# A shorter scan warm-up, A u as its own product, and zero products between scan steps

## The chip, the cores and the metric

The kernel runs on one core of one Trainium2 chip. The metric is the device time of one execution in microseconds (us), lower is better. The core has the engines PE (matrix products, with its weight loads listed as PEld), DVE (VectorE), ACT (ScalarE), POOL (GpSimd) and SP (which issues DMAs). PE's granted clock is given as a share of full speed; it is either 1.0 or 0.5 in a given window of 3.41 us.

## The reference

One block: layer norm, cross attention with 8 heads, a second layer norm, and a small state-space recurrence over 4096 positions, whose output is added to the residual. Cut to what matters here (T = 4096 positions, 3202 keys, H = 512, state S = 64):

```python
x  = residual + _mha(layernorm(x), layernorm(ctx), W_qkv, b_qkv, W_o, b_o)
xn = layernorm(x)
U  = (xn @ W_in.T + b_in) @ Bmat              # 4096 x 64

def step(s, u_t):
    s = silu(s @ A.T) + u_t
    return (s, s)
_, states = scan(step, zeros, U)              # one after the other, 4096 steps

x  = x + states @ Cmat
return x + (program_probs.mean(axis=1) @ W_prog.T + b_prog)
```

silu(z) is z times the logistic function of z; with z = 2 z', it is z' (tanh(z') + 1), which is what the kernel computes.

## The kernel before

**Attention.** The queries are 8 blocks of 512; a unit is one block, one pair of heads and one half (256 queries), 64 units in all. Each unit takes 13 chunks of 2 x 124 keys. For a chunk PE makes scores (L464), ACT copies them (L474), DVE keeps a running maximum (L485), later DVE subtracts the maximum (L519), ACT takes the exponent (L529), POOL accumulates the sums (L538) and PE multiplies by V (L547). The 832 steps (unit, chunk) are written out in one loop over g (L945), in which the later stages run some 16 steps behind the scores. For the last unit the sums of even chunks are made on PE instead (L563), those of odd chunks on POOL.

**The drain.** After the last scores (k = g - 832 counts from 0) only the subtract, exponent and V products of the last unit are left, with the scan's first steps put in at the values k of SCAN_AT (L940). fetch (L740) brings in, for k = 1 to 16, the rows of the residual that the output will be added to; last_fetch (L747) the constants.

**The projection.** finish, project (L623) and its copy for the last 256 rows, last_rows (L850), form x1 = residual + attention output (L859, L867), its layer norm, the transposes (L140) and u = 2 (W x + b) (L884, L891). For all rows but the last 256, u is ready before the drain.

**The scan.** It isn't run over 4096 steps. The positions are cut into 256 chunks of L = 16, 128 of them on the lower 64 partitions and 128 on the upper, so one step of all chunks is one product of 128 x 128 with a block-diagonal A. What a chunk starts from is found by running ahead: main_scan (L829) runs

- WARM = the last 8 steps of each chunk from the u before them (sweep at L837),
- a full sweep of 16 steps from the ends of the chunks to the left (L839),
- a second full sweep (L841), which also makes the output: products (L800, s @ Cmat, two products of 64 x 128 x 512) and outputs (ACT L805, DVE L806 and POOL L810 add them to the row, SP sends it out).

At the end, differ compares the two sweeps' ends; where they differ by more than 2^-21 of the maximum, a repair loop runs (under the condition at L1028). A step (L776) is the product z = A s (L778), tanh (L780), h = (tanh + 1) z (L781) and s = h + u (L782), each waiting for the one before.

**The last rows.** The last 256 positions have their u late, so they are a scan of their own (last_rows from L898): chunks of LT = 8 with PRE = 24 steps run ahead. Here z = A u is one product for all steps at first (zl, L900) and A h is added to it (L910), so a step needs no addition of u. Its 32 steps run beside the main scan's sweeps. last_outputs (L921) multiplies them by Cmat and adds.

**What sets the order.** Everything from L942 is a manual schedule: an engine executes its instructions in the order in which the program records them. Generators (`yield`) interleave last_rows with the scan, one scan step for each piece. When last_rows is exhausted, the rest of the scan runs alone (L1014), then last_outputs, the comparison and the end.

PSUM: z has two halves of 4 steps; py has two pairs of banks.

Of the kernel before, what the change touches and what calls it, by code (L numbers as in the profile page):

```python
# [8 lines left out]
F32 = mybir.dt.float32  # L9
BF16 = mybir.dt.bfloat16  # L10
I32 = mybir.dt.int32
AF = mybir.ActivationFunctionType
ALU = mybir.AluOpType
# [15 lines left out]
LAG = 3  # L29
EPS = 1e-5  # L30
L = 16
WARM = 8
LT = 8
PRE = 3 * LT
NCK = T // L // 2
TOL = 2.0**-21

# [10 lines left out]
def xattn_ssm_kernel(  # L48
# [34 lines left out]

    ident = const.tile([P, P], F32, name="ident")
    make_identity(nc, ident)
    ones = const.tile([P, HD], F32, name="ones")
    nc.vector.memset(ones, 1.0)
    neg_half = const.tile([P, 1], F32, name="neg_half")
# [482 lines left out]
    def finish_last(w):  # L571
        Q, hp, half = w["at"]
        o = op.tile([P, QU], F32, tag="o", name=f"o_{Q}_{hp}_{half}", bufs=12)
        o_t[Q, hp, half] = o
        nc.scalar.copy(o, w["po"][:, 0, :])
        sums(w["pd"], w["acc"], CK, False, True)
        yield
        rd = op.tile([P, QU], F32, tag="rd", name="rd_last", bufs=1)
        for t in range(2):
            nc.vector.reciprocal(  # L580
                rd[:, t * P : (t + 1) * P], w["pd"][:, t * P : (t + 1) * P]
            )
        nc.vector.tensor_tensor(o, o, rd, ALU.mult)
        yield

    def finish(w):

# [143 lines left out]

    x1r = x1d.rearrange("(v c j) o -> v j c o", v=2, j=L)
    outr = out.rearrange("(v c j) o -> v j c o", v=2, j=L)
    counts = (NCK, END)
# [10 lines left out]
    def last_fetch():  # L747

        for g in range(2):
            r = LAST + g * P  # L750
            t = xp_.tile([P, H], F32, tag="x", name=f"xr_{r}", bufs=3)
            nc.sync.dma_start(t, x[r : r + P, :])
            xl.append(t)
        t = qp.tile([P, QB], F32, tag="q", name="c2")
        for k in (0, NS):
            nc.sync.dma_start(t[k : k + NS], cmat)
        sv["c2"] = t
        one = sp_.tile([P, 8, NCK], F32, tag="s", name="scan_1")
        sv["th"] = [one[:, i, :] for i in range(2)]
        sv["h"] = [one[:, 2 + i, :] for i in range(2)]  # L760
        sv["s"] = [one[:, 4 + i, :] for i in range(3)]
        sv["ok"] = one[:, 7, :]
        two = sp_.tile([P, 1024], F32, tag="s", name="scan_2")
        at_ = 0
        for name, n in (
            ("end0", NCK + 1), ("end1", NCK + 1), ("ul", PRE + 1 + P), ("hw", P), ("hl", P),
            ("sl", P + 1), ("df", NCK), ("thl", P // LT), ("st", P // LT),
            ("top", 1), ("bad", 1), ("badl", 1),
        ):
            sv[name] = two[:, at_ : at_ + n]  # L770
            at_ += n
        assert at_ <= 1024
        for g in range(2):
            nc.gpsimd.tensor_tensor(xl[g], xl[g], rowb, ALU.add)

    def step(j, before, s, z):  # L776

        nc.tensor.matmul(z, a_t, before, start=True, stop=True)  # L778
        th, h = sv["th"][j % 2], sv["h"][j % 2]
        nc.scalar.activation(th, z, AF.Tanh, scale=0.5)  # L780
        nc.vector.scalar_tensor_tensor(h, th, 1.0, z, ALU.add, ALU.mult)  # L781
        nc.vector.tensor_tensor(s, h, u[:, j, :], ALU.add)  # L782

    def zs(j):
        return sv["z"][:, j // 4 % 2, j % 4, :]

    def sweep(first, start, end):

        before = start
        for j in range(first, L):  # L790
            s = end[:, 1:] if j == L - 1 else sv["s"][j % 3]
            step(j, before, s, zs(j))
            before = s
            yield j, s
        nc.vector.tensor_copy(end[NS:, 0:1], end[:NS, NCK : NCK + 1])

    def products(j, s):
        for v, n in enumerate(counts):
# [30 lines left out]
    def main_scan():  # L829
        ends = sv["end0"], sv["end1"]  # L830
        sv["z"] = ps_s.tile([P, 2, 4, NCK], F32, tag="s", name="z")
        for end in ends:
            nc.vector.memset(end[:NS, 0:1], 0.0)

        n = PRE + 1 - L
        nc.vector.tensor_copy(sv["ul"][:NS, :n], u[NS:, L - n :, END - 2])
        nc.vector.tensor_copy(sv["ul"][:NS, n : PRE + 1], u[NS:, :, END - 1])  # L837
        for _ in sweep(L - WARM, u[:, L - WARM - 1, :], ends[0]):
            yield  # L839
        for _ in sweep(0, ends[0][:, :NCK], ends[1]):  # L840
            yield  # L841
        for j, s in sweep(0, ends[1][:, :NCK], ends[0]):
            yield
            products(j, s)
            outputs(j)
            yield
        differ(ends[0][:, 1:], ends[1][:, 1:], NCK, sv["bad"])
        yield

    def last_rows(w):  # L850

        yield from finish_last(w)
        Q, tiles = NQB - 1, range(2)
        pas, x1s, scaled, xns = [], [], [], []
        for g in tiles:
            pa = ps_m.tile([P, H], F32, tag="m", name=f"pa_l{g}")
            pas.append(pa)
            for c in range(NC):
                nc.tensor.matmul(  # L859
                    pa, o_t[Q, c, 1][:, g * P : (g + 1) * P], wo[:, c, :],  # L860
                    start=(c == 0), stop=(c == NC - 1),
                )
            yield
        for g in tiles:
            x1 = xp_.tile([P, H], F32, tag="x1", name=f"x1_l{g}")
            x1s.append(x1)
            nc.vector.tensor_tensor(x1, pas[g], xl[g], ALU.add)  # L867
            scaled.append(normalize(x1, P, f"yl{g}", later=True))
            yield
        tps = []  # L870
        for g in tiles:
            xh = scaled[g]()
            tps.append(transposes(ps_m, "m", xh, P, f"yl{g}"))
            nc.gpsimd.tensor_tensor(xl[g], x1s[g], modb, ALU.add)
            yield
        pus = []
        for g in tiles:
            xn = sv["xn"][:, g, :].rearrange("p (c k) -> p c k", c=NC)
            nc.scalar.copy(xn, tps[g])
            hs = slice(g * NS, (g + 1) * NS)  # L880
            pu = ps_m.tile([P, P], F32, tag="m", name=f"pu_l{g}")
            pus.append(pu)
            for c in range(NC):
                nc.tensor.matmul(  # L884
                    pu[hs], wc[:, c, :], xn[:, c, :], start=(c == 0), stop=(c == NC - 1)
                )
            yield
        ul, hw, hl, sl, th = (sv[k] for k in ("ul", "hw", "hl", "sl", "thl"))
        for g in tiles:
            hs = slice(g * NS, (g + 1) * NS)  # L890
            nc.vector.tensor_scalar(  # L891
                ul[hs, PRE + 1 :], pus[g][hs], bu[hs], 2.0, ALU.add, ALU.mult
            )
            if g == 0:
                nc.vector.tensor_copy(ul[NS:, : PRE + 1], ul[:NS, P:])
            nc.sync.dma_start(x1d[LAST + g * P : LAST + (g + 1) * P, :], xl[g])

        zl = ps_m.tile([P, PRE // LT + 1, P], F32, tag="m", name="zl")  # L898
        for i in range(PRE // LT + 1):
            nc.tensor.matmul(  # L900
                zl[:, i, :], a_t, ul[:, i * LT : i * LT + P], start=(i == 0), stop=True,
                skip_group_check=True,
            )
        yield
        before = None
        for t in range(PRE + LT):
            i, j = divmod(t, LT)
            z = zl[:, i, j::LT]
            if before is not None:
                nc.tensor.matmul(z, a_t, before, start=False, stop=True, skip_group_check=True)  # L910
            h = (hl if i == PRE // LT else hw)[:, j::LT]
            nc.scalar.activation(th, z, AF.Tanh, scale=0.5)  # L912
            nc.vector.scalar_tensor_tensor(h, th, 1.0, z, ALU.add, ALU.mult)
            if t == PRE:

                nc.vector.tensor_tensor(sv["st"], hw[:, LT - 1 :: LT], ul[:, PRE :: LT][:, : P // LT], ALU.add)
            before = h
            yield
        nc.vector.tensor_tensor(sl[:, 1:], hl, ul[:, PRE + 1 :], ALU.add)
# [17 lines left out]
        nc.vector.tensor_copy(sl[:NS, 0:1], sv["end0"][NS:, END : END + 1])  # L937
        nc.vector.tensor_copy(sl[NS:, 0:1], sl[:NS, P:])

    SCAN_AT = (*range(1, 9), 10, 12, 14, 16)  # L940
    scan = main_scan()
    with tc.manual_schedule():  # L942
        for g in range(AHEAD):
# [64 lines left out]
                ps_o.tile([P, H], F32, tag="o", name="py_o"),  # L1008
            ],
        ]  # L1010
        end = last_rows(ws[len(units) - 1])
        next(end)
        for _ in end:
            next(scan, None)  # L1014
        for _ in scan:
            pass
        last_outputs("a")
        neighbours()
        differ(sv["sl"][:, : P : LT], sv["st"], P // LT, sv["badl"])
        pbad = ps_m.tile([P, H], F32, tag="m", name="pbad")  # L1020
# [7 lines left out]
    with tc.If(n > 0):  # L1028
        e = sv["end0"]
        with tc.For_i(0, 2 * NCK, 1):  # L1030
            for _ in sweep(0, e[:, :NCK], e):
                pass
        for j, s in sweep(0, e[:, :NCK], e):
            fetch(j)
            products(j, s)
            outputs(j)
        nc.vector.tensor_copy(sv["sl"][:NS, 0:1], e[NS:, END : END + 1])
        with tc.For_i(0, 2 * P // LT, 1):
# [70 lines left out]
```

## Time and profile before

| what | us |
|---|---|
| runs, median of 3 (lowest, highest) | 2654.03 (2651.61, 2657.15) |
| profiled execution, whole | 2654.64 |
| its span, first to last instruction | 2652.9 |
| PE busy in the span | 2511.1 (95%) |
| DVE busy | 2161.1 (81%) |
| POOL busy | 2073.8 (78%) |
| ACT busy | 1849.0 (70%) |
| mean granted clock of PE | 0.973 |

The end of the span falls into four stretches: the drain of the attention with the first scan steps (2482.0 to 2534.9), the preparation of the last 256 rows with further scan steps (to 2570.4, the first output product), the output sweep (to 2639.0) and a tail of comparisons and last stores (to 2652.9). Busy times of engines can overlap; a stage is set by the chain of waits in it, not by the sum of its busy times. Matmuls in f32 take several passes, so one product is several records in the trace ("x2", "x4", "x8").

### The profile page before, as it was taken

Reading aid. Unit: us, or ns where it says so; the run is one execution under the profiler, and the core shown is the slowest. Engines: PE = TensorE matmul, PEld = TensorE weight load, DVE = VectorE, ACT = ScalarE, POOL = GpSimd, SP = SyncE. Lnnn points to the kernel's source line nnn. Section 1 sums busy time; section 2 is a strip of 40 time slices with the busy share of each in tenths; the row PEclk is TensorE's granted clock in tenths of the full one; section 3 lists DMA queues with packets and bytes.
Section 4 is the critical chain, followed back from the end, with each engine's and each line's share of the span. In section 5 each row is a group of like instructions: output and inputs, shape, how many; then the busy total and the mean of one; then the engine's idle time right before and its main releaser. Section 6 shows DMA issues by size and latency. Waiting matters only on the chain.

```text
span 2652.9 us, 44604 instructions
## 1 busy us (share of the span) xinstructions
PE 2511.1 (95%) x16642; PEld 1433.9 (54%) x16642; DVE 2161.1 (81%) x2372; ACT 1849.0 (70%) x2133; POOL 2073.8 (78%) x1183
## 2 busy tenths in 40 slices
PE   7989899999999999999999999999999999999776
PEld 3445455555565556555655555555555565555443
DVE  2210797999979897999799989999799979999843
ACT  2232687877878787878787778778787878787521
POOL 1120497999979997999799988999799979999622
PEclk9999999999999999999999999999999999999865
DMA  4422221112211131122122211122121312333423
GB/s 126 136 87 74 71 68 49 51 57 84 59 45 54 54 88 33 55 63 74 43 58 62 72 51 51 57 84 59 47 60 51 85 35 75 112 111 105 130 75 105
DMA packets 178037, 189.24 MB, mean 71 GB/s; under 512 B 14252, under 2 KB 151256, under 8 KB 177818
## 3 DMA queue, kind: packets, MB, share of 16 engines
q1 hardware_dynamic: 173270, 178.67, 22.9%
q10 hardware_dynamic: 4548, 7.67, 0.9%
q8 instruction: 135, 2.21, 0.3%
q14 instruction: 84, 0.69, 0.1%
HBM read 156.40 MB, written 29.89 MB: 70 GB/s over the span
## 4 chain that ended last, share of the span: by engine, by line
PE 50%; DVE 28%; issue 11%; ACT 8%; DMA 1%; SPq 1%; POOL 0%; ACTq 0%; DVEq 0%
DVE top L485 17%; PE s L464 15%; PE po L547 13%; DVE p L519 6%; PE pq L179 4%; PE pa L635 4%; ACT p L474 4%; PE pv L393 3%; PE pk L419 3%; ACT p L529 2%; PE tt L496 2%; DVE rd L606 1%; PE mb L511 1%; PE pu L664 1%; DVE m L503 1%
## 5 line engine op out<-in xcount | busy, mean ns | idle before, releaser
L538 POOL TENSOR_TENSOR acc<-p,acc 123x1024 f32<-123x1024 f32 x698 | 1651.5, 2366 | 119.4 <-ACT p L529 77.2
L474 ACT COPY p<-s 123x1024 f32<-123x1024 f32 (+1 forms) x832 | 834.1, 1003 | 285.2 <-PE s L464 272.5
L464 PE MATMUL s<-q,k 64*123 64x256 f32 (+1 forms) x6656 | 943.2, 402 | 61.0 <-DVE top L485 48.0
L519 DVE TENSOR_TENSOR p<-p,mb 123x1024 f32<-123x1024 f32 (+1 forms) x832 | 1000.0, 1208 | 0.0
L529 ACT ACTIVATE p<-p 123x1024 f32<-123x1024 f32 (+1 forms) x832 | 880.2, 1058 | 160.0 <-DVE p L519 152.5
L485 DVE TENSOR_TENSOR top<-s,top 123x1024 f32<-123x1024 f32 x704 | 855.5, 1215 | 143.7 <-ACT p L474 135.3
L547 PE MATMUL po<-p,v 123*64 123x256 f32 (+1 forms) x6656 | 906.1, 393 | 4.2 <-ACT p L529 3.9
L464 PEld LDWEIGHTS s<-q,k 64*123 64x123 f32 (+1 forms) x6656 | 561.4, 182 | 374.3 <-DVE top L485 163.1
L547 PEld LDWEIGHTS po<-p,v 123*64 123x64 f32 (+1 forms) x6656 | 405.0, 136 | 403.8 <-issue 223.8
L538 POOL TENSOR_TENSOR acc<-p,p 124x1024 f32<-124x1024 f32 x64 | 151.7, 2371 | 154.4 <-ACT p L529 154.2
L119 POOL TENSOR_SCALAR ve_c<-mv_c 123x1 f32<-123x1 f32 (+1 forms) x26 | 5.8, 225 | 146.9 <-DVE mv_c L117 127.0
L179 PE MATMUL pq<-xn,wq 128*128 128x256 f32 x512 | 117.9, 383 | 0.0
L363 DVE COPY ct<-tp_c 128x492 f32<-128x492 f32 (+1 forms) x13 | 8.7, 671 | 128.0 <-PE tp_c L140 128.0
L635 PE MATMUL pa<-wo,o 128*128 128x512 f32 x240 | 111.0, 605 | 0.0
L485 DVE TENSOR_TENSOR top<-s,p 124x1024 f32<-124x1024 f32 x64 | 77.6, 1213 | 40.1 <-DMA k<-kd 38.8
L179 PEld LDWEIGHTS pq<-xn,wq 128*128 128x128 f32 x512 | 94.8, 190 | 20.5 <-issue 6.3
L393 PE MATMUL pv<-wv,ct 128*123 128x512 f32 (+1 forms) x208 | 97.7, 615 | 0.0
L427 ACT ACTIVATE ks<-pk,bias 128x492 f32<-128x492 f32 (+2 forms) x28 | 18.0, 642 | 112.5 <-PE pk L419 63.4
L419 PE MATMUL pk<-ct,wk 128*128 128x492 f32 (+2 forms) x224 | 89.2, 550 | 0.0
L595 POOL TENSOR_TENSOR both<-acc 124x512 f32<-124x512 f32 x63 | 80.7, 1282 | 4.9
L503 DVE TENSOR_REDUCE m<-tt 128x2 f32<-128x496 f32 x128 | 79.6, 661 | 0.7 <-PE tt L496 0.7
L810 POOL TENSOR_TENSOR row<-y_l,row 112x512 f32<-112x512 f32 x16 | 20.2, 1264 | 69.7 <-ACT scan L912 40.8
(171 smaller groups left out, 1469.9 us busy)
## 6 DMA issues: line engine op xcount, KB each, us to landing
k<-kd SPq DMA_DIRECT2D x396, 123.0 KB
v<-vd SPq DMA_DIRECT2D x396, 123.0 KB
k<-kd SPq DMA_DIRECT2D x72, 124.0 KB
v<-vd SPq DMA_DIRECT2D x72, 124.0 KB
xr<-in_x_dram SPq DMA_DIRECT2D x32, 256.0 KB
x1d<-xr SPq DMA_DIRECT2D x32, 256.0 KB
x<-in_x_dram SPq DMA_DIRECT2D x28, 256.0 KB
cx<-in_ctx_dram SPq DMA_DIRECT2D x22, 246.0 KB
```

Source lines behind the costliest of these rows:

```text
L179: nc.tensor.matmul(pq[:, half * QU : (half + 1) * QU], wq[:, i, hp * P : (hp + 1) * P], xns[half][:, i, :], start=(i == 0), stop=(i == NC ...
L393: nc.tensor.matmul(pv[:n, :H], ct[:, i, o : o + n], wv[:, i, :], start=(i == 0), stop=(i == NC - 1),)
L419: nc.tensor.matmul(pk[:, :n_g], wk[:, i, hp * P : (hp + 1) * P], ct[:, i, :n_g], start=(i == 0), stop=(i == NC - 1),)
L464: nc.tensor.matmul(s[:n, a, b, :], kts[(*w["at"][:2], c)][r, b * n : (b + 1) * n], q[r], start=True, stop=True,)
L474: nc.scalar.copy(t[:n], s[:n])
L485: nc.vector.tensor_tensor(w["top"][:n], s[:n], before[:n], ALU.max)
L503: nc.vector.tensor_reduce(m[:, t, :], tps[t].rearrange("p a b k -> p a (b k)"), AX.X, ALU.max)
L519: nc.vector.tensor_tensor(t[:n], t[:n], w["mb"][:n].unsqueeze(2).to_broadcast([n, 2, 2, QU]), ALU.subtract,)
L529: nc.scalar.activation(t[:n], t[:n], AF.Exp)
L538: nc.gpsimd.tensor_tensor(w["acc"][:n], t[:n], before[:n], ALU.add)
L547: nc.tensor.matmul(w["po"][a * HD : (a + 1) * HD, 0, :], vts[(*w["at"][:2], c)][:n, b, a * HD : (a + 1) * HD], t[:n, a, b, :], start=(c == ...
L635: nc.tensor.matmul(pa, o_t[Q, c, t // 2][:, t % 2 * P : (t % 2 + 1) * P], wo[:, c, :], start=(c == 0), stop=(c == NC - 1),)
```

## The change

- WARM goes. The first sweep is a full sweep of 16 steps that starts from zero states (its first h is set to zero), and the second one makes the output. So a chunk is run ahead by 16 steps and not by 24.
- A u is a product of its own for 4 steps at a time (`terms`), and A h is added to it in PSUM, as the last rows had it already. A step is now product, tanh and h; the state s = h + u is an addition on POOL (`states`), made only in the output sweep, where the products wait for it.
- outputs(j - 1) is recorded after step j and before the state of step j.
- SCAN_AT has 4 entries, so four pieces of the scan stand in the drain where there were twelve. After the drain, three scan steps stand behind the first pieces of the last rows' projection, whose products are split so that those that need the last unit's result come after these.
- The last rows run ahead 16 steps (PRE) and not 24. Their output (last_outputs("a")) is recorded when they are done, before the rest of the output sweep.
- In the first sweep, from the end of the drain on, two bf16 products of zeros (128 x 128 by 128 x 512) follow each step's product, except where the terms are made. Their results are never read.

```diff
-WARM = 8
-PRE = 3 * LT
+PRE = 2 * LT
...
+    zeros = const.tile([P, H], BF16, name="zeros")
+    nc.gpsimd.memset(zeros, 0.0)
...
-    def step(j, before, s, z):
-        nc.tensor.matmul(z, a_t, before, start=True, stop=True)
-        th, h = sv["th"][j % 2], sv["h"][j % 2]
-        nc.scalar.activation(th, z, AF.Tanh, scale=0.5)
-        nc.vector.scalar_tensor_tensor(h, th, 1.0, z, ALU.add, ALU.mult)
-        nc.vector.tensor_tensor(s, h, u[:, j, :], ALU.add)
...
+    def terms(q, start):
+        z = sv["z"][:, q % 2]
+        if q:
+            nc.tensor.matmul(z, a_t, u[:, 4 * q - 1 : 4 * q + 3, :], start=True, stop=True)
+            return
+        if start is not None:
+            nc.tensor.matmul(z[:, 0, :], a_t, start, start=True, stop=True)
+        nc.tensor.matmul(
+            z[:, 1:, :], a_t, u[:, :3, :], start=start is None, stop=True,
+            skip_group_check=True,
+        )
+
+    def sweep(start, end, fill=0):
+        before = None
+        for j in range(L):
+            if j == 0:
+                terms(0, start)
+            h = sv["h"][j % 3]
+            z = sv["z"][:, j // 4 % 2, j % 4, :]
+            if before is not None:
+                nc.tensor.matmul(z, a_t, before, start=False, stop=True, skip_group_check=True)
+            if j % 4 == 1 and j + 4 < L:
+                terms(j // 4 + 1, None)
+            elif "fill" in sv:
+                for _ in range(fill):
+                    nc.tensor.matmul(
+                        sv["fill"], zeros[:, :P], zeros, start=True, stop=True
+                    )
+            if j == 0 and start is None:
+                nc.vector.memset(h, 0.0)
+            else:
+                th = sv["th"][j % 2]
+                nc.scalar.activation(th, z, AF.Tanh, scale=0.5)
+                nc.vector.scalar_tensor_tensor(h, th, 1.0, z, ALU.add, ALU.mult)
+            before = h
+            if j < L - 1:
+                yield j, h
+        nc.vector.tensor_tensor(end[:, 1:], h, u[:, L - 1, :], ALU.add)
         nc.vector.tensor_copy(end[NS:, 0:1], end[:NS, NCK : NCK + 1])
+        yield j, h
+
+    def states(j, h):
+        s = sv["s"][j % 2]
+        nc.gpsimd.tensor_tensor(s, h, u[:, j, :], ALU.add)
+        return s
...
-        for _ in sweep(L - WARM, u[:, L - WARM - 1, :], ends[0]):
+        for _ in sweep(None, ends[1], 2):
             yield
-        for _ in sweep(0, ends[0][:, :NCK], ends[1]):
+        for j, h in sweep(ends[1][:, :NCK], ends[0]):
+            if j:
+                outputs(j - 1)
             yield
-        for j, s in sweep(0, ends[1][:, :NCK], ends[0]):
+            products(j, states(j, h))
             yield
-            products(j, s)
-            outputs(j)
-            yield
+        outputs(L - 1)
...
     def last_rows(w):
-        yield from finish_last(w)
+        finish_last(w)
...
+        pas = sv["py"][0]
+        for part in (range(NC - 1), range(NC - 1, NC)):
+            for g in tiles:
+                for c in part:
+                    nc.tensor.matmul(
+                        pas[g], o_t[Q, c, 1][:, g * P : (g + 1) * P], wo[:, c, :],
+                        start=(c == 0), stop=(c == NC - 1),
+                    )
             yield
...
-    SCAN_AT = (*range(1, 9), 10, 12, 14, 16)
+    SCAN_AT = (1, 2, 3, 4)
...
-        end = last_rows(ws[len(units) - 1])
-        next(end)
-        for _ in end:
-            next(scan, None)
+        sv["fill"] = sv["py"][1][0]
+        last = last_rows(ws[len(units) - 1])
+        for i, _ in enumerate(last):
+            for more in range(3 if i == 0 else 1):
+                next(scan, None)
+        last_outputs("a")
         for _ in scan:
             pass
-        last_outputs("a")
         neighbours()
```

More of the change, by code (lines that the diff above doesn't have):

```diff
@@ L583, in finish_last @@
         nc.vector.tensor_tensor(o, o, rd, ALU.mult)
-        yield
     def finish(w):
@@ L759, in last_fetch @@
         sv["th"] = [one[:, i, :] for i in range(2)]
-        sv["h"] = [one[:, 2 + i, :] for i in range(2)]
-        sv["s"] = [one[:, 4 + i, :] for i in range(3)]
+        sv["h"] = [one[:, 2 + i, :] for i in range(3)]
+        sv["s"] = [one[:, 5 + i, :] for i in range(2)]
         sv["ok"] = one[:, 7, :]
@@ L774, in last_fetch @@
             nc.gpsimd.tensor_tensor(xl[g], xl[g], rowb, ALU.add)
-    def step(j, before, s, z):
-        nc.tensor.matmul(z, a_t, before, start=True, stop=True)
-        th, h = sv["th"][j % 2], sv["h"][j % 2]
[L780 to L794, printed above, removed]
-        nc.vector.tensor_copy(end[NS:, 0:1], end[:NS, NCK : NCK + 1])
+    def terms(q, start):
[9 more added lines that the diff above has]
+        )
@@ L837, in main_scan @@
         nc.vector.tensor_copy(sv["ul"][:NS, n : PRE + 1], u[NS:, :, END - 1])
-        for _ in sweep(L - WARM, u[:, L - WARM - 1, :], ends[0]):
+        for _ in sweep(None, ends[1], 2):
             yield
-        for _ in sweep(0, ends[0][:, :NCK], ends[1]):
+        for j, h in sweep(ends[1][:, :NCK], ends[0]):
+            if j:
+                outputs(j - 1)
             yield
-        for j, s in sweep(0, ends[1][:, :NCK], ends[0]):
+            products(j, states(j, h))
             yield
-            products(j, s)
-            outputs(j)
-            yield
+        outputs(L - 1)
         differ(ends[0][:, 1:], ends[1][:, 1:], NCK, sv["bad"])
@@ L850, in last_rows @@
     def last_rows(w):
-        yield from finish_last(w)
+        finish_last(w)
         Q, tiles = NQB - 1, range(2)
[L854 to L862, printed above, removed]
+        x1s, scaled = [], []
+        pas = sv["py"][0]
[6 more added lines that the diff above has]
+                    )
             yield
@@ L1030, in xattn_ssm_kernel @@
         with tc.For_i(0, 2 * NCK, 1):
-            for _ in sweep(0, e[:, :NCK], e):
+            for _ in sweep(e[:, :NCK], e):
                 pass
-        for j, s in sweep(0, e[:, :NCK], e):
+        for j, h in sweep(e[:, :NCK], e):
             fetch(j)
-            products(j, s)
+            products(j, states(j, h))
             outputs(j)
```

## The prediction

> **What bounds the kernel now.** I read the page's slices first: PE is busy 95% of the span, and its last slices fall to 7, 7, 6 tenths with the clock down to 0.5. The order of instructions on each engine is the same in both kernels up to the last unit's drain (PE, ACT, DVE), so the change lives in the last 171 us. I cut them by the stretches of drain, preparation of the last rows, output sweep and tail (columns: window, length, then busy time and count on PE, PEld, DVE, ACT, POOL, then clock, DMA share, GB/s):
>
> ```profile
> 2482.00:2534.90 52.90, 37.52 (x230) 20.24 (x228) 37.98 (x50) 20.16 (x31) 27.25 (x13) 0.81 0.59 173
> 2534.90:2570.40 35.50, 23.38 (x81) 16.11 (x80) 14.60 (x43) 6.47 (x21) 4.61 (x8) 0.65 0.04 15
> 2570.40:2639.00 68.60, 58.05 (x152) 29.32 (x154) 25.08 (x76) 16.78 (x58) 18.97 (x15) 0.50 0.31 108
> 2639.00:2652.90 13.90, 2.08 (x8) 0.29 (x6) 6.89 (x25) 0.60 (x1) 1.26 (x1) 0.62 0.22 77
> ```
>
> No engine is full in the drain, and the output sweep runs at half clock. Next, the granted clock in single windows:
>
> ```profile
> 2484.32:2487.74 3.42, 1.50 (x10) 0.78 (x10) 3.35 (x7) 0.87 (x1) 3.42 (x3) 1.00 0.70 202
> 2487.74:2491.15 3.41, 1.11 (x4) 0.71 (x4) 3.38 (x4) 1.41 (x3) 3.33 (x2) 0.50 0.40 107
> 2504.80:2508.22 3.42, 3.42 (x16) 2.33 (x18) 2.03 (x4) 1.22 (x2) 0.79 (x1) 0.50 0.59 178
> 2528.70:2532.11 3.41, 1.98 (x18) 0.81 (x13) 2.25 (x2) 2.19 (x3) 1.06 (x1) 1.00 0.75 198
> 2542.35:2545.76 3.41, 0.77 (x5) 0.39 (x3) 2.50 (x8) 0.55 (x2) 0.38 (x2) 1.00 0.00 0
> 2545.76:2549.18 3.42, 2.28 (x8) 1.75 (x8) 1.95 (x6) 0.98 (x2) 2.29 (x6) 0.50 0.00 0
> ```
>
> The clock falls after a window with PE busy 1.50 or 0.77 us, holds after 1.98, and comes back only after one that was full. From 2545.8 on it is down. Last, the groups in the drain and one cycle of the output sweep in order of time:
>
> ```profile
> L519 DVE TENSOR_TENSOR p<-p,mb 123x1024 f32<-123x1024 f32 x14 | 16.6, 1208 | 0.0
> L782 DVE TENSOR_TENSOR scan<-scan,u 128x128 f32<-128x128 f32 x12 | 12.9, 1072 | 0.7
> ...
> 2598.61 0.50 PEld L910 LDWEIGHTS zl<-scan,a_t 128*128 128x128 f32 x2 [1.50 <-issue]
> 2598.78 0.60 ACT L805 ACTIVATE y_l<-py 128x512 f32<-128x512 f32 x1 [2.64 <-PE py L800]
> 2599.05 0.78 PE L778 MATMUL z<-scan,a_t 128*128 128x128 f32 x2
> 2599.45 1.27 POOL L810 TENSOR_TENSOR row<-y_l,row 112x512 f32<-112x512 f32 x1 [3.14 <-ACT scan L912]
> 2599.87 0.28 ACT L780 ACTIVATE scan<-z 128x128 f32<-128x128 f32 x1 [0.42 <-PE z L778]
> 2600.18 0.29 DVE L781 SCALAR_TENSOR_TENSOR scan<-scan,z 128x128 f32<-128x128 f32 x1
> 2600.50 0.37 DVE L782 TENSOR_TENSOR scan<-scan,u 128x128 f32<-128x128 f32 x1
> 2600.92 1.22 PE L800 MATMUL py_b<-c,scan 64*128 64x512 f32 x1
> ```
>
> In the drain the 12 adds of u cost 1072 ns each where 290 is their bare time: DVE is the queue that binds. In the output sweep the loop is py 2.08, z 0.78, tanh, stt, add, next py. Over 15 steps (68.6 - 2.08)/15 = 4.43 us each; POOL's row add lies beside it, unused by the chain.
>
> **The skill.** "TensorE: Matmul & The Clock Gate", Part 1: The HAM clock gate, says that PE's clock is half or full by windows of 3.4 us. The trace agrees on the window (3.41) and the two values; the page lets it fall after an idle window, here 0.77 and 1.50 us of work did not hold it, and the trace decides. Same page, Back-to-back issue gap: a bf16 product of 512 columns takes 216 ns warm and 427 cold by its formula; this is my price for a filler, since before has none. "SBUF - State Buffer", Who interferes with whom: a DVE operation with two SBUF inputs contends with GpSimd's reads, one with at most one does not. The trace agrees: L782 (both in SBUF) takes 0.29 alone and up to 2.36 beside POOL, L781 (one input in PSUM) stays at 0.285.
>
> **Term 1, drain.** Four scan steps stand in it in place of twelve. DVE loses 8 or more L782 (about 8 x 1.07 = 8.6 us), 8 stt (2.3), ACT 8 tanh, PE 8 products with their waits. PE then ends last: POOL's chain of the unit before (three accumulations, two xr adds, three accumulations, "both": 7.2 + 2.6 + 7.2 + 1.3, back to back) frees the sums' input at about 2495.4, and from 2495.9 PE has 11 po groups x 0.95 + 7 groups of sums x 0.87 (both at the full-clock durations of the drain's records) + 1.1 for pd and rb = 17.6 and some 0.3 between them, so 2513.9. The windows near 2491-2494 are thin and I expect one cold stretch, +3: T0, the end of the last sums, at 2516.8 in place of 2534.9: **-18**. Bounds: no cold stretch gives 2514; row fetches compressed against v loads (59% DMA share of 52.9 us is 31 us of full queues, in 35) give up to 2520.
>
> **Term 2, preparation (T0 to the first py).** It still has the chain pa, x1, normalize, transpose, pu, ul, zl, with about one first-sweep step beside each. The fillers (2 after each step's product, PE's clock held by them) change its clock: warm, 6 pa products 6 x 0.86 = 5.2 (four took 3.44 in before's preparation, at full clock), three steps and two more products end at T0+10.0; x1 11.2; the normalized tiles (1.6 us after their statistics, one after the other on DVE) 14.4 and 16.4; transposes 0.65 each, 17.3; pu, 1.0 each (1.97 in the cold of before), with a step between, 22.2; ul 24.2; three zl products (four before) 25; steps 14 and 15 and the copy of the ends 27.7; z and stt of the first output step 28.8; its state and py at T0+29.4. Before: 35.5. **-6.1**. A step lost its L782 from the chain: from z to next z 0.49 + 0.28 + 0.29 + hand-overs = 1.18 warm, and z plus two fillers fill 0.92 of it, so they are hidden; cold, 0.80 + 0.85 = 1.65 against 1.5 would show 0.15 a step. The A u products for 4 steps (0.86 for 512 columns) stand where no filler does.
>
> **Term 3, output sweep.** Here the order decides. POOL's queue is: row add of step j-1, then the new state add of step j, and py(j) waits for the state. ACT's queue is tanh(j), then y_l(j-1). So the chain takes in what lay beside it: from py start, 2.08 py and 0.37 zl, z 0.77, 0.04, then 0.17 into tanh ACT begins y_l, 0.60, 0.08, row add 1.27, 0.04, state, 0.07, next py. The state add of 128 columns is not in the trace: POOL's 512 columns take 1.275 and 1024 take 2.366, a slope of 0.27 per 128, hence 0.45. Bounds 0.3 (POOL's smallest operation is 0.225) and 0.8 (a hand-over more than I see). Sum 5.94, and 5.5 once the last rows' zl steps have ended. Its PE stream is thin: with no fillers here the clock holds one or two windows and falls; warm steps would be 4.5. So 4.5 + 5.3 + 9 x 5.95 + 4 x 5.5 + 1.65 (the last rows' product, moved between) = 87.0, plus the last py 2.08: 89.1 against 68.6, **+20.5**. The state's bounds put -2 and +5 on it.
>
> **Term 4, tail.** The two L929 (1.29) now come earlier, so 12.4 for 13.9: **-1.5**. The zeros' memset falls in POOL's idle start (its first long work begins at 8.3): 0. PRE at 16 takes 8 zl steps off the last rows, which run beside the output sweep: in the 5.5 above.
>
> **Sum.** -18 - 6.1 + 20.5 - 1.5 = -5.1. The profiled execution of before took 2654.64 (span 2652.9); the median of the runs is 2654.03. So about **2649**. The measurement of this kernel can tell 0.2%, 5.3 us; my forecast is at that bound, since two large terms cancel.
>
> **Rivals.**
> - *The clock holds in the output sweep too.* Steps of 4.5 where I have 5.9: 18 us less, about 2631. For: z, zl and py together keep PE busy for some 1.9 of 4.5 us warm, close to the 1.98 of 3.41 that held. Against: that is 1.4 of 3.41, below the 1.50 that did not.
> - *The clock is lost in the preparation* (the slower side). Place: the stretch from the last pa to the transposes, where before lost it too (0.77 busy). If a window catches it with too few fillers, no window afterwards is full enough to bring it back. Price: 7.9 for the stages computed cold (pu, tp, zl, A u and z at twice the time), 2 for the output sweep's warm start, and 0.15 for each of some ten steps with fillers: 11.4, so 2660. It decides when the loss exceeds 10.4 (5.1 + 5.3). For: two fillers in a step of 1.2 to 2 us lie at 0.9 us of PE work per step, and steps stand only one to each piece of the chain, up to 3 us apart. Against: fillers stream at full width.
> - *The drain is held by transfers or POOL*, T0 5 later than I have it, 2654: no change. For: the DMA share. Against: no v wait in the drain of before.
> - *It doesn't do what it says*: the ends differ after 16 steps by more than the tolerance and the repair runs. In float64 on the reference's inputs I find a difference of 9.4e-9 after 16 steps, tolerance 4.8e-7 of the maximum: under 1%.
>
> **Chances.** My sum 0.62 (faster by over 0.2% 0.38, within 0.20, slower 0.04; alone 2643 to 2656); output sweep warm 0.12; clock lost 0.15, all slower; drain held 0.10 (within 0.09, slower 0.01); repair under 0.01. Faster 0.50, same 0.29, slower 0.21. The range 2638 to 2661 leaves out the warm output sweep and the ends of the others.
>
> **What would show it.** Drain: last sums by 2517, PE without long waits on DVE. Preparation: clock 1.0 up to the first py, 29 us after T0. Output sweep: py to py 5.9, the state add starting at the row add's end on POOL, clock 0.5 after two windows. It is wrong if the state does not wait for the row add, if the output sweep's clock is 1.0, or if T0 comes after 2521.

## The result and the profile after

The changed kernel takes 2660.41 us (median of 9 runs, 2657.97 to 2661.31), the kernel before 2653.39 (9 runs, 2651.19 to 2657.15): a ratio of 1.0023 with a 95% interval of [1.0013, 1.0033]. It is 7 us slower, where 5 us faster was forecast. The profiled execution took 2659.27 with a span of 2657.0, 4.1 more than the span of before, and 0.5 more outside it. It lies 1.1 under its median and the profiled one of before 1.25 over its own, which is the rest of the 7.

The same four stages, cut at the ends of the last scores, of the last sums (T0) and at the first and last output product:

| stage | before | forecast | after |
|---|---|---|---|
| drain, last scores to T0 | 57.1 | -18 | 48.1 (-9.0) |
| preparation, T0 to first py | 35.5 | -6.1 | 31.0 (-4.5) |
| output sweep, to the end of the last py | 68.6 | +20.5 | 91.7 (+23.1) |
| tail, to the end of the span | 13.9 | -1.5 | 9.9 (-4.0) |
| everything ahead of the last scores | 2477.8 | 0 | 2476.4 (-1.4) |

The busy times by stretch of the changed kernel (same columns as in the prediction: window, length, PE, PEld, DVE, ACT, POOL, clock, DMA share, GB/s):

```profile
2474.00:2524.40 50.40, 36.19 (x255) 20.32 (x253) 29.11 (x35) 23.16 (x27) 33.63 (x16) 0.90 0.60 173
2524.40:2555.40 31.00, 23.33 (x104) 12.69 (x102) 10.36 (x30) 6.29 (x20) 5.01 (x9) 1.00 0.10 36
2555.40:2647.20 91.80, 56.81 (x146) 26.41 (x146) 20.17 (x58) 14.27 (x51) 25.24 (x30) 0.55 0.25 86
2647.20:2657.00 9.80, 0.38 (x4) 0.17 (x4) 5.65 (x22) 0.60 (x1) 1.26 (x1) 0.50 0.16 54
```

The clock is full through the preparation (1.00, before 0.65): the zero products did their work. The output sweep is as cold as before (0.55) and PE's busy time in it is nearly the same (56.81 against 58.05), so all of the 23 us are waits. And the drain moves no more GB/s than before although it was meant to be shorter.

The drain of the changed kernel in order of time, PE's V products and SP's DMA issues (start, length, engine, line, and in brackets the idle time ahead of it with what ended it):

```profile
2501.92 0.42 SPq L693 DMA_DIRECT2D v<-vd  x1
2502.25 1.03 PE L548 MATMUL po<-p,v 123*64 123x256 f32 x8
2502.89 2.39 SPq L745 DMA_DIRECT2D row<-x1d  x2
2505.09 1.08 PE L548 MATMUL po<-p,v 123*64 123x256 f32 x8 [1.81 <-DMA v<-vd]
2505.64 0.24 SPq L693 DMA_DIRECT2D v<-vd  x1
2506.36 2.46 SPq L745 DMA_DIRECT2D row<-x1d  x2
2508.63 1.08 PE L548 MATMUL po<-p,v 123*64 123x256 f32 x8 [1.59 <-DMA v<-vd]
2509.18 0.24 SPq L693 DMA_DIRECT2D v<-vd  x1
2510.03 3.77 SPq L745 DMA_DIRECT2D row<-x1d  x4
2512.16 1.36 PE L548 MATMUL po<-p,v 123*64 123x256 f32 x8 [2.44 <-DMA v<-vd]
```

SP issues in order: a row fetch (two DMAs, 480 KB), then a V load (123 KB), then a row again, one pair for each drain step. In the drain of before the same pair looks like this:

```profile
2504.80 0.81 SPq L745 DMA_DIRECT2D row<-x1d  x2
2505.66 0.30 SPq L694 DMA_DIRECT2D v<-vd  x1
```

With the faster drain steps two row issues take 2.4 us in place of 0.81, and each V load starts behind them; what lengthens an issue was not tested. PE, which had no wait on V in the drain of before, waits for it five times, 8.9 us in all. What that does to the clock stands in the windows that follow:

```profile
2505.79:2509.21 3.42, 1.83 (x18) 1.19 (x16) 0.00 (x0) 0.89 (x1) 2.63 (x2) 1.00 0.58 173
2509.21:2512.62 3.41, 0.97 (x11) 0.46 (x9) 0.00 (x0) 0.00 (x0) 0.00 (x0) 1.00 0.53 169
2512.62:2516.03 3.41, 2.60 (x14) 1.36 (x10) 0.00 (x0) 0.00 (x0) 0.00 (x0) 0.53 0.94 261
2519.45:2522.86 3.41, 2.63 (x14) 1.69 (x16) 0.00 (x0) 0.37 (x1) 0.00 (x0) 0.50 0.72 207
```

A window with 0.97 us of PE work costs the clock for the 10 us up to 2522.9. DVE, which the prediction read as the binding engine of before, does nothing in these windows (0.00).

A step of the output sweep, in order of time:

```profile
2572.34 1.22 PE L829 MATMUL py_b<-c,scan 64*128 64x512 f32 x1 [2.12 <-POOL scan L823]
2574.79 0.78 PE L799 MATMUL z<-scan,a_t 128*128 128x128 f32 x2
2575.60 0.28 ACT L812 ACTIVATE scan<-z 128x128 f32<-128x128 f32 x1 [0.43 <-PE z L799]
2575.78 0.59 ACT L834 ACTIVATE y_l<-py_o 128x512 f32<-128x512 f32 x1
2575.98 0.29 DVE L813 SCALAR_TENSOR_TENSOR scan<-scan,z 128x128 f32<-128x128 f32 x1 [0.59 <-ACT scan L812]
2576.45 1.26 POOL L839 TENSOR_TENSOR row<-y_l,row 112x512 f32<-112x512 f32 x1 [4.16 <-ACT scan L941]
2577.67 0.46 POOL L823 TENSOR_TENSOR scan<-scan,u 128x128 f32<-128x128 f32 x1
2578.18 2.08 PE L829 MATMUL py<-c,scan 64*128 64x512 f32 x4 [2.12 <-POOL scan L823]
```

h (the line of L813) is there at 2576.27, but the state (L823) starts at 2577.67, when POOL has ended the row add of the step before (L839). From py to py 5.84 us. Two of the steps take 7.54; in them an A u product stands between z and tanh:

```profile
2580.63 0.78 PE L799 MATMUL z<-scan,a_t 128*128 128x128 f32 x2
2581.20 1.91 PE L780 MATMUL z<-u,a_t 128*128 128x512 f32 x2
2583.15 0.28 ACT L812 ACTIVATE scan<-z 128x128 f32<-128x128 f32 x1 [2.14 <-PE z L780]
```

### The profile page after: what moved, and what is told of

Same layout as the page of the kernel before. It is cut to its first block, busy times and chain, and to the rows that moved or that the text cites. A ratio compares the mean times of both kernels' runs of the same rounds, so it can differ in the third digit from the quotient of the medians.

```text
span 2657.0 us, 44549 instructions
## 1 busy us (share of the span) xinstructions
PE 2500.8 (94%) x16642; PEld 1423.7 (54%) x16642; DVE 2135.8 (80%) x2317; ACT 1845.4 (69%) x2116; POOL 2082.9 (78%) x1200
## 4 chain that ended last, share of the span: by engine, by line
PE 48%; DVE 27%; issue 13%; ACT 8%; DMA 2%; SPq 1%; POOL 1%; ACTq 0%; DVEq 0%; POOLq 0%
DVE top L486 17%; PE s L465 15%; PE po L548 13%; DVE p L520 6%; PE pq L180 4%; PE pa L634 4%; ACT p L475 4%; PE pv L394 3%; ACT p L530 2%; PE pk L420 2%; PE tt L497 2%; DVE rd L605 1%; PE mb L512 1%; PE pu L663 1%; DVE m L504 1%
## 5 line engine op out<-in xcount | busy, mean ns | idle before, releaser
L180 PEld LDWEIGHTS pq<-xn,wq 128*128 128x128 f32 x512 | 94.8, 190 | 20.5 <-issue 6.3
L839 POOL TENSOR_TENSOR row<-y_l,row 112x512 f32<-112x512 f32 x16 | 20.2, 1264 | 67.3 <-ACT scan L941 44.4
```

What stands on the lines that cost most here:

```text
L180: nc.tensor.matmul(pq[:, half * QU : (half + 1) * QU], wq[:, i, hp * P : (hp + 1) * P], xns[half][:, i, :], start=(i == 0), stop=(i == NC ...
```

## The experiments

### The drain: rows after the V loads

```diff
-            if 0 < k <= L:
-                fetch(k - 1)
+            if k >= 12:
+                for j in range(3 * (k - 12), min(3 * (k - 11), L)):
+                    fetch(j)
```

> The changed kernel with the 16 row fetches recorded after the last V loads (three per drain step from k = 12) in place of one per step from k = 1; nothing else moves. Theory (V loads stand behind row fetches in SP's queue and in the transfers, 8.9 us of PE waits on V in the drain of the changed kernel): these waits go, the last sums end 6 to 8.5 us earlier against the last scores (39.5 to 42 us after them, 48.3 in the changed kernel), time 2652 to 2655. Rival (the drain is then held by POOL or by ACT at the same point, or the late rows delay the first output step): the last sums end less than 2 us earlier, or a wait on a row comes up in the output sweep, time 2658 to 2662.

Measured: 2645.66 us, 0.9973 of before [0.9962, 0.9983], 14.7 less than the changed kernel and below the range expected. PE has no wait on V left, and T0 comes 34.7 us after the last scores in place of 48.1. That is 13.4 less where the waits named were 8.9: without them no window went thin, and the clock stayed full to the end of the sums. The rest of the kernel kept its times (preparation 31.0, sweep 91.1), and no output step waited for a row. The V waits and the clock lost with them, 13.4 us, more than cover the 9 us by which the drain missed its forecast.

The same edit in the kernel before:

> The kernel before with the row fetches after the last V loads, as in the changed kernel's version of this; nothing else moves. Theory (the drain of before is held by DVE, with 12 additions of u blocked by POOL, and no V load came late in it): the last sums stay at 55 to 58 us after the last scores, time 2650 to 2656. Rival (the row fetches held the drain of before too, in a way that its waits don't name): last sums below 53, time below 2649.

Measured: 2654.01 us, 0.9999 of before [0.9990, 1.0008], T0 at 57.1 as before. The same fetches in the same place cost nothing in the slower drain of before.

One part of the change alone, in the kernel before:

```diff
-    SCAN_AT = (*range(1, 9), 10, 12, 14, 16)
+    SCAN_AT = (1, 2, 3, 4)
```

> The kernel before with SCAN_AT = (1, 2, 3, 4): eight scan steps moved from the drain to behind it, nothing else. Theory (with the scan out of the way the drain is held by V loads behind the row fetches): the last sums end 46 to 52 us after the last scores in place of 57.5, with 5 to 10 us of PE waits on V where there were none; eight steps of 1.9 us come back behind the drain, time 2655 to 2661. Rival (only this change's other parts let V come late): no V waits, last sums within 42 us, time under 2652.

Measured: 2664.57 us, 1.0041 of before [1.0027, 1.0055], above the range. T0 comes at 50.5, with V waits of 6.1 us where there were none, as expected of the theory; T0 to the first py goes from 35.5 to 51.9. So moving eight steps out of the drain gains 6.6 and costs 16.4 in the kernel before, and this part of the change alone is enough to make V late. It takes the work of eight steps off PE, ACT and DVE together; that DVE was the one that had slowed the drain is read from the trace of before (its additions of u at 1072 ns) and was not tested alone.

### The output sweep: the state before the row add

```diff
         for j, h in sweep(ends[1][:, :NCK], ends[0]):
+            s = states(j, h)
             if j:
                 outputs(j - 1)
             yield
-            products(j, states(j, h))
+            products(j, s)
             yield
```

> The changed kernel with the state's addition recorded before the outputs of the step before, so that POOL's queue is state, then row add; PE, ACT and DVE keep their order. Theory (the state stands behind y_l and the row add on POOL, which is what lengthens a step from 4.4 to 5.84 us): py to py becomes 2.08 + 0.37 + 0.77 + 0.04 + 0.28 + 0.03 + 0.29 + 0.05 + 0.46 + 0.05 = 4.4 us at half clock, 15 steps x 1.4 = 21 less, 2638 to 2642. Rival (POOL is the bound by its two additions and hand-overs, or DVE's row operations hold the state back): steps stay above 5.3, time above 2652.

Measured: 2641.64 us (one of four runs 2632.86), 0.9947 of before [0.9926, 0.9967]: 18.8 less than the changed kernel, as expected. The end of the chain in a step, in order of time:

```profile
2562.24 0.29 DVE L813 SCALAR_TENSOR_TENSOR scan<-scan,z 128x128 f32<-128x128 f32 x1 [2.23 <-ACT scan L812]
2562.61 0.45 POOL L823 TENSOR_TENSOR scan<-scan,u 128x128 f32<-128x128 f32 x1 [5.70 <-DVE scan L813]
2563.02 1.26 POOL L839 TENSOR_TENSOR row<-y_l,row 112x512 f32<-112x512 f32 x1
2563.11 0.28 PEld L829 LDWEIGHTS py_b<-c,scan 64*128 64x128 f32 x1 [1.09 <-POOL scan L823]
```

The state now starts 0.08 us after h, and the row add lies beside py. Steps at half clock beside the last rows take 4.55 to 4.62 us, and three at full clock, which came back by itself here, some 3.15. The sweep takes 73.0 in place of 91.7: the one exchange on POOL gives back 18.7 of the 23.1 us, part of it through the clock of these steps.

### The output sweep: the A u products after h

```diff
-            if j % 4 == 1 and j + 4 < L:
-                terms(j // 4 + 1, None)
-            elif "fill" in sv:
+            more = j % 4 == 1 and j + 4 < L
+            if not more and "fill" in sv:
...
+            if more:
+                terms(j // 4 + 1, None)
             before = h
```

> The changed kernel with the A u products for the next 4 steps recorded after tanh and h of the step instead of before them; PE keeps its order. Theory (tanh waits for the A u product although it reads the other half of z, 1.7 us at half clock in 3 steps of the output sweep and about 0.7 in 3 steps of the first sweep, of which two stand after the drain): steps of 7.54 become 5.84 to 5.9, 3 x 1.7 = 5.1, and 1 to 1.5 in the preparation, so 2653 to 2656. Rival (the A u product lies on PE's path to the next product anyway): the 7.5 us steps stay within 0.4, time 2659 to 2661.

Measured: 2659.82 us, 1.0025 of before [1.0014, 1.0035]: no gain. The time is the rival's, but not its reason: the two steps of 7.54 did fall, to 6.23, and the drain took 52.1 in place of 48.1. PE's waits in it name why (wait, us in total, times, longest):

```profile
PE po L548 <- DMA v<-vd: 7.9, 5, 2.6
PE z L780 <- DVE scan L811: 3.3, 1, 3.3
```

The wait was turned round: recorded behind h, the A u product waits for DVE's h, which reads the tile that it writes to, although in its other half; in the drain DVE comes to h late. That both waits come from z being one tile is argued from these two orders; two tiles weren't tried.

### The clock in the output sweep

```diff
-            elif "fill" in sv:
-                for _ in range(fill):
+            if "fill" in sv and (start is not None or j % 4 != 1 or j + 4 >= L):
+                for _ in range(2):
                     nc.tensor.matmul(
-                        sv["fill"], zeros[:, :P], zeros, start=True, stop=True
+                        sv["py"][j % 2][0] if start is not None else sv["fill"],
+                        zeros[:, :P], zeros, start=True, stop=True
                     )
```

> The changed kernel with two zero products after each z product of the output sweep too (into the py bank that is written next; after the A u product where there is one). Theory (the half clock costs 1.4 us of each step of the output sweep; two fillers per step of 4.5 keep PE busy for some 2.4 of 4.5 us and hold the clock): clock 1.0 through the sweep, steps of 4.3 to 4.6, sweep from the first py to the last 66 to 71 us in place of 91.7, time 2638 to 2644. Rival (windows still come too thin and the clock falls in the sweep as before): steps of 5.84 and more, time 2659 to 2664.

Measured: 2654.35 us, 1.0005 of before [0.9996, 1.0013], well above the range and below the rival's. The steps at full clock take 4.38, so the price of the clock was right (1.46 a step), but only the first steps and a later one had it. The clock first fell in the sweep behind the second of these windows:

```profile
2559.68:2563.09 3.41, 2.21 (x12) 1.21 (x12) 0.21 (x2) 0.59 (x3) 1.14 (x2) 1.00 0.42 144
2563.09:2566.50 3.41, 1.37 (x8) 0.52 (x7) 1.04 (x3) 0.43 (x2) 1.68 (x2) 1.00 0.40 139
2566.50:2569.92 3.42, 1.91 (x8) 1.38 (x7) 1.26 (x4) 1.13 (x4) 1.68 (x2) 0.51 0.14 55
```

A mean of 2.4 us of work per step of 4.5 did not hold it: work and waits fall unevenly on the windows, and the one ahead of the fall had 1.37 of 3.41. Fillers in a loop that waits for POOL leave its wait as it is.

### The zero products

```diff
-        for _ in sweep(None, ends[1], 2):
+        for _ in sweep(None, ends[1], 0):
```

> The changed kernel without the zero products. Theory (the fillers are what holds the clock through the preparation): the clock falls within two windows after the last projection products, transposes, pu, A u and z take twice the time, T0 to the first py goes from 31.1 to 36 to 40 us, and the first output step is cold too; time 2666 to 2670. Rival (the real products hold the clock, or the chain is ACT's and DVE's): T0 to the first py stays within 1.5 us, time 2659 to 2662.

Measured: 2667.61 us, 1.0055 of before [1.0038, 1.0072], 7.2 more than with them. The preparation takes 35.0; its windows:

```profile
2537.29:2540.70 3.41, 1.62 (x6) 0.79 (x7) 2.40 (x7) 0.98 (x2) 1.97 (x6) 1.00 0.00 0
2540.70:2544.11 3.41, 1.50 (x13) 1.12 (x11) 0.57 (x2) 1.73 (x4) 2.57 (x3) 1.00 0.21 79
2544.11:2547.53 3.42, 2.60 (x10) 1.98 (x10) 0.29 (x1) 0.75 (x2) 0.00 (x0) 0.52 0.20 77
```

The clock fell behind the window with 1.50 us of real work; with two fillers a step the changed kernel keeps it through this stretch, where its thinnest window (2536.7 to 2540.1) has 1.91. So 4.0 of the 7.2 us lie in the preparation and 0.8 in the sweep's colder start; 2.1 more lie behind the last instruction of the engines' own work, where the profile names nothing.

### Both edits together, and a step further

Rows after V and the state ahead of the row add, together:

> Row fetches after the last V loads and the state before the row add on POOL, together. Theory (two separate terms in separate stretches, measured at -14.7 and -18.8 alone): they add, 2624 to 2630. Rival (the later rows or the row adds that follow the states closely get into each other's way: a row that comes late holds the first output steps): 2632 or more.

Measured: 2623.27 us, 0.9886 of before [0.9870, 0.9903]. The two add (2626.9 would be the plain sum) and a little more comes, as about half of the output steps now run at full clock (2.9 to 3.4 us).

Then, on top of these, py behind the next z (the z-ahead kernel from here on):

```diff
             s = states(j, h)
+            yield
             if j:
+                products(j - 1, ready)
                 outputs(j - 1)
-            yield
-            products(j, s)
+            ready = s
             yield
+        products(L - 1, ready)
         outputs(L - 1)
```

> As the one with both, and in the output sweep the products of a state are recorded one step later, behind the next step's z. Theory (what is left in a step is the chain py, z, tanh, h, state, py, although z does not need the state; without it PE has no wait left, and a PE without waits gets its clock back): at half clock 2.08 + 0.78 + 1.2 = 4.1 a step while the last rows' steps run and 2.9 after, at full clock bounded by POOL's 0.46 + 1.26 + hand-overs, 1.8 to 2.2; the sweep 35 to 58 us from first to last py in place of 71, time 2595 to 2615. Rival (the row's DVE and ACT operations or the 16 output stores set the pace): steps above 4.2, time above 2620.

Measured: 2600.94 us, 0.9801 of before [0.9785, 0.9818]: the fastest but for a variant below that can't be told from it, 59.5 us under the changed kernel. Its stretches:

```profile
2478.60:2513.20 34.60, 29.40 (x237) 17.19 (x237) 26.69 (x32) 21.15 (x25) 31.35 (x15) 1.00 0.67 171
2513.20:2545.40 32.20, 24.69 (x110) 13.82 (x110) 10.53 (x31) 6.49 (x22) 5.01 (x9) 1.00 0.45 115
2545.40:2587.80 42.40, 33.68 (x139) 15.79 (x138) 20.30 (x56) 14.32 (x50) 25.31 (x30) 0.92 0.50 175
2587.80:2597.70 9.90, 0.38 (x5) 0.17 (x4) 5.69 (x22) 0.60 (x1) 1.31 (x2) 0.62 0.32 107
```

The output sweep takes 42.4 us where it took 91.7, with POOL busy for as long as in the changed kernel (25.31 and 25.24) and PE at 33.68 for 56.81, since the clock is 0.92. Steps are 2.5 to 3.0 us while the last rows run beside them, which is more than the 1.8 to 2.2 expected at full clock, and 1.7 to 2.2 after them.

The same without the zero products in the first sweep:

> The one with the products behind the next z, without the zero products in the first sweep. Theory (the fillers' worth is the preparation's clock, 4 us, and the clock with which the output sweep starts; this sweep now streams enough to win it back): preparation 34 to 37 us in place of 32.2, the first two to four output steps at half clock (4 in place of 3), time 2605 to 2610. Rival (the dense output sweep doesn't win the clock back without them): all steps with the last rows at 4 or more, time above 2613.

Measured: 2618.16 us, 0.9850 of before [0.9823, 0.9877]. The preparation takes 39.1, longer than expected, and the first eight output steps take 3.6 to 5.1 us: the rival was right, though one of its four runs took 2605.92. The fillers are worth 17 us here and 7 in the changed kernel; in the profiled executions 6.9 of it lies in the preparation and 11.8 in the output sweep (54.2 for 42.4).

Two further edits on the z-ahead kernel, the A u products after h (as above) and the last rows' output products three pieces later:

```diff
-        last_outputs("a")
-        for _ in scan:
-            pass
+        for i, _ in enumerate(scan):
+            if i == 3:
+                last_outputs("a")
```

> The one with the products behind the next z, with the A u products recorded after tanh and h, and the last rows' output products three pieces of the scan later. Theory (in the one before, one step took 5.27 us since PE waited 1.63 for the last rows' state sum and lost its clock for two windows; tanh waits for the A u product in two or three steps): that step below 4, the clock full to the end of the sweep, sweep 37 to 40 us in place of 42.4, time 2595 to 2599. Rival (the wait moves to the stores or to the row adds on POOL): within 1.5 of 2600.9.

Measured: 2617.39 us, 0.9851 of before [0.9829, 0.9872]: 16 worse, not better. In its drain the A u product waits 3.3 us for h, as in the run with these products after h above, and these are the windows:

```profile
2484.80:2488.22 3.42, 0.49 (x2) 0.30 (x2) 3.39 (x6) 1.22 (x2) 3.42 (x4) 0.95 0.20 67
2488.22:2491.63 3.41, 2.83 (x6) 1.03 (x8) 0.52 (x2) 1.06 (x1) 3.33 (x2) 0.50 0.14 47
```

T0 comes at 39.4, and the clock falls again in the preparation and in the sweep. The later output products alone:

> The one with the products behind the next z, with the last rows' output products three pieces of the scan later, and the A u products where they were. Of the two parts of the run at 2617 this is one alone. Theory (that run lost its time to the A u products behind h: in its drain PE waits 3.3 us on DVE's h for the A u product, a window goes nearly empty, and the clock falls there and again later): without that part the last sums end 34 to 36 us after the last scores, the 5.27 us step falls below 4, time 2595 to 2600. Rival (the late output products are what hurts): sweep above 45 us, time above 2605.

Measured: 2599.69 us, 0.9795 of before [0.9779, 0.9812], T0 at 34.7. So the A u products behind h were what hurt. The later output products themselves gain nothing that can be told: the step of 5.27 is gone, but in this execution the clock fell for four windows at the sweep's start (sweep 44.0).

## Why the prediction was wrong

**The drain (forecast -18, measured -9.0): the step that failed.** "PE then ends last" counted only what PE does. V coming late stood among the rivals at 0.10, with "no v wait in the drain of before" against it. That argument doesn't hold: the drain of before took 57 us, slowed by DVE as its trace reads, and V loads behind 480 KB of rows per step were in time for that pace. In the faster drain the same queue order costs waits of 8.9 us, and the thin window costs the clock on top. The run with the rows later shows the sum itself: 34.7 us after the last scores where the term had 39.0, so with the transfers out of the way it was too pessimistic (I had put 3 us on a cold stretch that then doesn't occur). The rival's price of 5 us was too low too: T0 came 9 later than my term. The waits are 8.9 of it, and the cold stretch behind them took the 4.3 that the term had in hand.

**The preparation (forecast -6.1, measured -4.5).** Fillers hold the clock: right, shown by the run without them (35.0). Two of them take 0.59 us in the trace. 1.6 us are missing. About as much is seen where tanh waits for the A u product in two of its steps, 1.39 us from z's start to tanh in place of 0.48, which I had not put on the chain. That this is the 1.6 is argued: the run with these products after h has the next z behind them instead of tanh, and its preparation takes 31.5.

**The output sweep (forecast +20.5, measured +23.1).** The chain through POOL was right, its step 5.84 for 5.94, the state add 0.46 for 0.45. What lacked is one term: the A u products of this sweep, 1.7 us in each of two steps at half clock and some 0.8 in the first step, at full clock (5.24 us, where the run with fillers in this sweep has steps of 4.38 without one). They appear in the prediction's account of the first sweep, and not here. The first two steps took 11.1 for 9.8: 5.24 for 4.5 with that A u product, and 5.84 for 5.3, already cold. The last four took 21.0 for 22.

**The tail (forecast -1.5, measured -4.0).** From the last py to the cast of the count 6.4 us for 7.7, as forecast. The other 2.8 lie behind the cast, 3.5 to the end of the span for 6.2, and no run tested what they are. They need not come from the change: with the same instructions in the tail, this part took 5.6 in two variants (fillers in the output sweep, and no fillers at all).

**The rivals.** The clock was not lost in the preparation, the repair did not run (no instruction of it is in the trace), the output sweep did not keep its clock. The slower outcome came by two terms that I had small or not at all, 9 us in the drain and some 4 of A u in the output sweep, less 2.5 in the tail. That the rival with the clock lost in the preparation was priced at 2660 as well is chance: what it describes did not happen.

## What to carry to other kernels

Before an engine is relieved, ask of every queue beside it how fast it must go afterwards: a transfer that is never waited for may be in time only because the binding engine is slow. Where work is taken off one engine and put on another, read the order of the receiving engine's queue: on POOL an addition of 0.46 us started 1.4 us late in a step because it stood behind another of 1.26. And what waits for nothing should be recorded ahead of what waits: z before py, V before rows.

## What the runs showed of the hardware

PE's clock was lost behind windows of 3.41 us with PE busy for 0.97, 1.37 and 1.50, and not behind one of 1.83. "TensorE: Matmul & The Clock Gate", Part 1: The HAM clock gate, of the Trainium skill names an idle window for the fall; here partly busy ones were enough.

PE's busy time in a window is not the whole rule, though. In the run with both edits the clock was lost behind a window with 2.49 us:

```profile
2550.71:2554.12 3.41, 2.49 (x15) 1.43 (x13) 1.16 (x4) 1.02 (x4) 1.81 (x3) 1.00 0.58 208
2554.13:2557.54 3.41, 2.58 (x9) 1.34 (x8) 1.25 (x4) 1.02 (x4) 1.68 (x2) 0.50 0.36 121
```

And in the output sweep of the changed kernel it did not come back behind one in which the trace has PE busy throughout:

```profile
2604.96:2608.37 3.41, 3.41 (x10) 2.03 (x8) 0.18 (x1) 0.34 (x2) 0.00 (x0) 0.50 0.00 0
2608.38:2611.79 3.41, 1.04 (x3) 0.51 (x4) 1.07 (x3) 0.68 (x3) 1.68 (x2) 0.50 0.34 118
```

It came back in the changed kernel behind one with 2.81 (2519.6 to 2523.0) and in the kernel before behind one with 2.80 (2637.9 to 2641.3). What else counts was not tested.

In the z-ahead kernel zero products far from the output sweep are worth 17 us, most of it in the sweep (42.4 us, and 54.2 without them), which starts at the full clock that they held. Without them three of the four executions took 2618 us or more, and one 2605.92.
